# Layer 1's feed-forward in rounds of scores, full products and values, and patches loaded image by image

## The chip, the cores and the metric

The kernel runs on one NeuronCore of one Trainium2 chip. A core has five engines that run beside each other: TensorE (PE in the profile; its weight loads are PEld), VectorE (DVE), ScalarE (ACT), GpSimd (POOL) and SyncE (SP, which here only starts transfers). Matmuls read SBUF and write PSUM, which has eight banks of 512 float32 columns on 128 partitions. The metric is the time on the device, in microseconds, from the first to the last instruction of the program; the median of three runs of the kernel before is 2376.61 us (2375.67 to 2379.23).

## The reference

A small vision model on 32 images of 3 x 256 x 256 in float32. Each image becomes 256 tokens of 256 features (16 x 16 patches times a 768 x 256 matrix), and then passes two layers, each an attention and a feed-forward with a residual. The change touches the tokenizer and the feed-forward of layer 1, which is itself an attention: four heads of 64 features, with four experts each. Cut to what matters:

```python
h = patches @ W.T + b                                   # tokenizer, 32 x 256 tokens
...                                                     # layer 0, attention of layer 1
x = layernorm(h)
sx = x @ hl_w.T + hl_b                                  # 4 heads (n) of 64 features
q  = sx @ wq.T                                          # 4 experts (e) for each head
k, v = sx @ wk.T, sx @ wv.T
scores = q @ k.T * sqrt(64) + causal                    # 256 x 256 for each n and e
out = softmax(scores) @ v
gs  = softmax(concat_e(out) @ gate_w.T + gate_b)        # weight of each expert
mixed = sum_e out * gs
hn  = layernorm(mixed + resid)                          # over 64 features
hx  = relu(hn @ fc1_w.T + fc1_b) @ fc2_w.T + fc2_b
y   = layernorm(hx + hn)
fg  = softmax(y @ fgate_w.T)                            # weight of each head
h   = h + y * fg
```

## The kernel before

The program is written in steps; a scheduler places the instructions on the engines, roughly in program order. All matmuls are float32 and go through one helper, `mm(o, lhsT, rhs)`, so the profile shows one line (L113) for them all; tile names tell them apart. A float32 matmul leaves two records.

The tokenizer takes two images at a time, and all weights of layer 0 are loaded beside the first patches, on another queue:

```python
tokW = load(pw, "tokW")
row_a = load_rows(pw, "rows_a", ...)
wuv = load(wpool_b, "wuv")                # and rows_b, wo, rows_c, w1, w2, before, places
...
def unit_a(b0):
    x = px.tile([P, n_k, 2 * N], F32, name="patch")                 # three buffers
    nc.sync.dma_start(x, patches[:, :, b0 * N : (b0 + 2) * N])
    for j in range(2):
        p = bank()
        for c in range(NC):
            for k in range(n_k):
                mm(p[:, c * D : (c + 1) * D], x[:, k, o : o + P], tokW[:, k, :], k == 0, k == n_k - 1)
        ...                                # bias, statistics of the rows
```

After each half of the images `finish_a` makes the row factors of 16 images at once, on VectorE and with square roots on ScalarE.

In layer 1's feed-forward an image passes through numbered steps, and six images are under way at a time, six steps apart. `prep` makes the operands, `scores` and `weights` the exponentials, `values` the weighted sums, `post` the rest:

```python
def prep(b, im, i):
    # i == 0: normalise, transpose          -> im.xT
    # i == 1: 4 matmuls of 256 columns      -> im.sx (ScalarE)
    # i in (2, 3): 4 matmuls of 256 with A  -> im.g  (half ScalarE, half VectorE)
    # i == 4: 4 matmuls of 168 columns      -> im.v ("ev", VectorE), count of zeros in sx

def scores(im, k):                          # k = 0..5; 64 partitions: two matmuls side by side
    hp, part = k // 3, k % 3
    for h in range(2):
        s, p = slice(h * HD, (h + 1) * HD), bank()
        if part < 2:
            mm(p, im.sx[s, hp, 0:P], im.g[s, hp, 2 * part : 2 * part + 2, :])
        else:
            mm(p, im.sx[s, hp, P:N], im.g[s, hp, :, P:N])

def weights(im, k):                         # mask on VectorE, exponential on ScalarE -> "et"
    for h in range(2):
        nc.vector.tensor_tensor(own, own, over(tri, [P, n_e, P], 1), ALU.add)
        nc.scalar.activation(t.rearrange("p e n -> p (e n)"), p, AF.Exp)

def values(im, j):                          # 64 output partitions: two matmuls side by side
    for n, c in (((2 * hp, 0), (2 * hp + 1, 0)), ((2 * hp, 1),), ((2 * hp + 1, 1),))[part]:
        p = bank()
        for e in range(NE):
            for m in range(c + 1):
                for q in (slice(0, HD), slice(HD, P)):
                    mm(p[q, e * VC : (e + 1) * VC], t[:, q], im.v[:, m, n * VC : (n + 1) * VC], m == 0, m == c)
        nc.scalar.copy(im.o[:, c * NH + n, 0 : NE * VC], p[:, 0 : NE * VC])
```

`VC` is 84: 64 columns of the head, and for each of the four experts four gate logits and a one, which gives the denominator. Every expert's product carries all 84.

```python
def post(b, im, i):
    # 0..2: denominators ("rden"), gates; at 2 GpSimd multiplies all outputs by the gates ("eo")
    # 3..5: sum of experts ("two", "er"), squares, factor by a power on GpSimd ("hv"), scaling
    # 6..8: transposes, fc1 ("hx"), fc2 with the centring matrix ("ey"), squares
    # 9..13: factor, scaling, transposes ("foT"), gate product ("fo_w"), "fout", store

PREP, POST = 6, 15
for t in range(6 * (B - 1) + POST + 14):
    active = [(b, t - 6 * b) for b in range(B) if 0 <= t - 6 * b < POST + 14]
    # for all active images: scores at i = 6..11, then post at 15..28, prep at 0..5,
    # weights at 6..11, values at 9..14
```

So each of the six steps of an image has scores of one image (two matmuls of 512 columns), full 128 x 128 products, and 16 value matmuls.

Of the kernel before, what the change touches and what calls it, by code (L numbers as in the profile page):

```python
# [37 lines left out]
P = 128  # L40
# [11 lines left out]
for _name, _k in [  # L52
    ("b_u", 4), ("b_base", 1), ("gamma", 2), ("beta", 2), ("b1", 8), ("bk1", 2), ("bq1", 2),
    ("bk2", 1), ("bq2", 1), ("ln_w", 2), ("ln_b", 2), ("hl_b", 2), ("fc1_b", 1), ("freq", 1),
    ("e_g", 1), ("e_b", 1), ("fn_g", 1), ("fn_b", 1),
]:
    COLS[_name] = (_n, _k)
    _n += _k
# [12 lines left out]
ROWS_B, N_ROWS_B = _rows(("b_v", 512), ("b_o", 256), ("g", 1))  # L71
# [7 lines left out]
def vit_tower(tc, a, out):  # L79
# [21 lines left out]
    def load_rows(pool, name, at, n):  # L101

        t = pool.tile([P, n], F32, name=name)
        nc.scalar.dma_start(t, a[name].partition_broadcast(P))
        return lambda x: t[:, at[x][0] : at[x][0] + at[x][1]]
# [89 lines left out]
    late = []  # L195

    def phase(unit, images, finish=None, every=1):

        active, step = [], 0
        todo = list(range(0, B, images))
        while todo or active:
            if todo and step % every == 0:
                b = todo.pop(0)
                active.insert(0, (b, unit(b)))
            step += 1
            for b, g in list(active):
                if next(g, g) is not g:  # L210
                    continue
                active.remove((b, g))
                while late:
                    late.pop(0)()
                if finish is not None and (b + images) % HALF == 0:
                    late.append(lambda k=b // HALF: finish(k))
# [7 lines left out]
    with tc.tile_pool(name="a_w", bufs=1) as pw, tc.tile_pool(name="a_x", bufs=3) as px:  # L224
        tokW = load(pw, "tokW")
        row_a = load_rows(pw, "rows_a", ROWS_A, N_ROWS_A)
        wuv = load(wpool_b, "wuv")
        row_b = load_rows(wpool_b, "rows_b", ROWS_B, N_ROWS_B)
        wo = load(wpool_b, "wo")
        row_c = load_rows(wpool, "rows_c", ROWS_C, N_ROWS_C)  # L230
        w1 = load(wpool, "w1")
        w2 = load(wpool, "w2")
        before = load(wpool, "before")
        places = load(wpool, "places")
        st_b = new_stats("b")
        n_k = tokW.shape[1]
        patches = a["patches"].rearrange("(k p) t -> p k t", p=P)

        def unit_a(b0):
            x = px.tile([P, n_k, 2 * N], F32, name="patch")  # L240
            nc.sync.dma_start(x, patches[:, :, b0 * N : (b0 + 2) * N])
            for j in range(2):
                b = b0 + j
                p = bank()
                for c in range(NC):
                    for k in range(n_k):
                        o = j * N + c * P
                        mm(p[:, c * D : (c + 1) * D], x[:, k, o : o + P], tokW[:, k, :], k == 0, k == n_k - 1)
                nc.vector.tensor_tensor(
                    H[b], p.rearrange("p (c d) -> p c d", c=NC), over(row_a("tok_b"), [P, NC, D], 1), ALU.add  # L250
                )
                st, _, i = at(st_b, b)
                for c in range(NC):
                    stats(st, i, c, H[b][:, c, :])
            yield

        def finish_a(k):


            st, rs = st_b[k]  # L260
            n = HALF * NC
            var = st.rearrange("p i c s -> p (i c) s")[:, :, 1]
            low = spool.tile([P, n], F32, name="low")
            v = rsqrt(low, var, 1e-5)
            nc.vector.scalar_tensor_tensor(low, low, 1e-5, v, ALU.mult, ALU.mult)
            s = spool.tile([P, n], F32, name="root")
            nc.scalar.activation(s, var, AF.Sqrt)
            nc.vector.tensor_scalar(s, s, 1e-18, None, ALU.max)
            r = spool.tile([P, n], F32, name="root_r")
            nc.vector.reciprocal(r, s)  # L270
            nc.vector.tensor_mul(r, r, var)
            nc.vector.tensor_add(s, s, r)
            nc.vector.scalar_tensor_tensor(s, s, 0.5, low, ALU.mult, ALU.max)
            nc.vector.reciprocal(r, s)
            nc.vector.tensor_scalar(rs, r, row_b("g"), None, ALU.mult)

        phase(unit_a, 2, finish_a)
# [95 lines left out]
    VC = HD + NE * (NE + 1)  # L373
    OC = NE * (VC + NE + 1)

# [49 lines left out]
    def prepare():  # L425
# [14 lines left out]
        for t in (A, WV, ones_row, fc2):  # L440
            nc.gpsimd.memset(t, 0.0)
        nc.gpsimd.memset(
            ones_row.rearrange("p (n x) -> p n x", n=NH)[:, :, HD:VC]
            .rearrange("p n (e x) -> p n e x", e=NE)[:, :, :, NE : NE + 1], 1.0,
        )
# [15 lines left out]
        for i in range(2):  # L461
# [4 lines left out]
            for hp in range(2):  # L466
                w = WV[s, hp, i * VC : (i + 1) * VC]
                nc.vector.tensor_copy(w[:, 0:HD], wv_i[s, hp, :])
                nc.vector.tensor_copy(
                    w[:, HD:].rearrange("p (e x) -> p e x", e=NE)[:, :, 0:NE],  # L470
                    pv[s, hp * 16 : hp * 16 + 16].rearrange("p (e x) -> p e x", e=NE),
                )

# [291 lines left out]
    with (  # L765
        tc.tile_pool(name="e_1", bufs=1, reuse_waits="tile") as p1,
        tc.tile_pool(name="e_2", bufs=2, reuse_waits="tile") as p2,
        tc.tile_pool(name="e_4", bufs=4, reuse_waits="tile") as p4,
    ):
        class Image:  # L770
            pass
# [3 lines left out]
        def prep(b, im, i):  # L775
            if i == 0:
                im.xT = features(p2, b)
            if i == 1:
# [10 lines left out]
            if i in (2, 3):  # L789
                hp = i - 2  # L790
# [5 lines left out]
            if i == 4:  # L796
# [12 lines left out]
            if i == 5:  # L809
                im.o = p2.tile([P, NC * NH, OC], F32, name="eo")  # L810

        def scores(im, k):


            hp, part = k // 3, k % 3
            if part == 0:
                im.t = getattr(im, "t", {})
                for h in range(2):
                    im.t[2 * hp + h] = (
                        p4.tile([P, NE, N], F32, name="et0"), p4.tile([P, NE, P], F32, name="et1"),  # L820
                    )
            im.p = []
            for h in range(2):
# [5 lines left out]
                im.p.append(p)  # L829

        def weights(im, k):

            hp, part = k // 3, k % 3
            for h in range(2):
                p, n_e = im.p[h], 4 if part == 2 else 2
                own = p.rearrange("p (e n) -> p e n", e=n_e)[:, :, 0:P]
                nc.vector.tensor_tensor(own, own, over(tri, [P, n_e, P], 1), ALU.add)  # L837
                t0, t1 = im.t[2 * hp + h]
                t = t1 if part == 2 else t0[:, 2 * part : 2 * part + 2, :]
                nc.scalar.activation(t.rearrange("p e n -> p (e n)"), p, AF.Exp)  # L840

        def values(im, j):
            hp, part = j // 3, j % 3
            for n, c in (((2 * hp, 0), (2 * hp + 1, 0)), ((2 * hp, 1),), ((2 * hp + 1, 1),))[part]:
                p = bank()
                t0, t1 = im.t[n]
                for e in range(NE):
                    for m in range(c + 1):
                        t = t1[:, e, :] if m else t0[:, e, c * P : (c + 1) * P]
                        for q in (slice(0, HD), slice(HD, P)):  # L850
                            mm(p[q, e * VC : (e + 1) * VC], t[:, q], im.v[:, m, n * VC : (n + 1) * VC], m == 0, m == c)
                nc.scalar.copy(im.o[:, c * NH + n, 0 : NE * VC], p[:, 0 : NE * VC])  # L852
# [26 lines left out]

        def post(b, im, i):  # L880
            if i == 0:
                by_e = im.o.rearrange("p g (e x) -> p g e x", e=NE)
                im.rden = spool.tile([P, NC * NH, NE], F32, name="rden")
                nc.vector.reciprocal(im.rden, by_e[:, :, :, HD + NE])
                nc.vector.scalar_tensor_tensor(good, im.rden, 1.0 / LOW, good, ALU.is_le, ALU.mult)
                nc.vector.scalar_tensor_tensor(good, im.rden, 1.0 / HIGH, good, ALU.is_ge, ALU.mult)
                lg = spool.tile([P, NC * NH, NE, NE], F32, name="lg")
                nc.vector.tensor_tensor(
                    lg, by_e[:, :, :, HD : HD + NE], over(im.rden, [P, NC * NH, NE, NE], 3), ALU.mult
                )  # L890
# [6 lines left out]
            if i == 2:  # L897
                softmax_rest(im.gate, NC * NH)
                nc.vector.tensor_tensor(im.gate, im.gate, im.rden, ALU.mult)  # L899
                im.by_e = im.o[:, :, 0 : NE * VC].rearrange("p g (e x) -> p g e x", e=NE)[:, :, :, 0:HD]  # L900
                nc.gpsimd.tensor_tensor(  # L901
                    im.by_e, im.by_e, over(im.gate, [P, NC * NH, NE, HD], 3), ALU.mult
                )
            if i == 3:
                two = p1.tile([P, NC * NH, 2, HD], F32, name="two")
                nc.vector.tensor_tensor(two, im.by_e[:, :, 0:2, :], im.by_e[:, :, 2:4, :], ALU.add)  # L906
                im.r = p2.tile(G8, F32, name="er")
# [12 lines left out]
            if i == 6:  # L920
                p = feature_major(im.r.rearrange("p (c n) d -> p c (n d)", c=NC))
                im.fT = p2.tile([P, 2, N], F32, name="fxT")
# [3 lines left out]
            if i == 7:  # L926
# [3 lines left out]
                im.hx = p2.tile([P, 2, N], F32, name="hx")  # L930
# [5 lines left out]
            if i == 8:  # L936
# [6 lines left out]
                im.r = p2.tile(G8, F32, name="ey")  # L943
# [4 lines left out]
            if i == 11:  # L948
                p = feature_major(im.r.rearrange("p (c n) d -> p c (n d)", c=NC))
                im.fT = p2.tile([P, 2, N], F32, name="foT")  # L950
# [16 lines left out]
            if i == 13:  # L967
                softmax_rest(im.gate, NC)
                y = p2.tile([P, NC, D], F32, name="fout")
# [10 lines left out]

        images = [Image() for _ in range(B)]
        PREP, POST = 6, 15
        for t in range(6 * (B - 1) + POST + 14):
            active = [(b, t - 6 * b) for b in range(B) if 0 <= t - 6 * b < POST + 14]
            for b, i in active:
                if PREP <= i < PREP + 6:
# [406 lines left out]
```

## Time and profile before

| stage | from, us | to, us |
|---|---|---|
| tokenizer | 13.2 (first matmul) | 182.1 |
| layer 0, attention and feed-forward | 182.1 | about 1026 |
| layer 1, attention | about 1026 | about 1400 |
| layer 1, feed-forward | about 1400 | 2376.4 |

The dearest groups of the last stage by the page, whole run (busy time, mean of one):

| group | count | busy us | mean ns |
|---|---|---|---|
| exponentials, ScalarE, 128x512 | 384 | 227.9 | 604 |
| value matmuls, 84 columns | 6144 records | 265.9 | 240 |
| score matmuls, 512 columns | 768 records | 218.6 | 641 |
| mask added, VectorE | 384 | 185.1 | 514 |
| outputs times gates, GpSimd, 128x2048 | 32 | 115.9 | 3620 |

Busy time is the union of the records of a group; matmul records overlap, since the next one starts while the one before is still in the array, so what a matmul costs is read from one start to the next. A wait is put down to the instruction that ended it.

### The profile page before, as it was taken

To read this page: it belongs to the slowest core of one execution; us is meant where nothing else is said; L and a number is where in the kernel's file an instruction comes from. 1 tells how busy PE (TensorE), PEld (TensorE's weight loads), DVE (VectorE), ACT (ScalarE), POOL (GpSimd) and SP (SyncE) were. 2 spreads that over 40 slices of the span, in tenths; PEclk is the share of its full clock that TensorE was granted. 3 is DMA by queue.
4 is the path that set the end of the run, shared out by engine and by line. 5 is a ranking of instruction groups with operands and counts; after the bars stand their busy time and mean duration, and the time that the engine had idled before them with its cause. 6 is when DMAs were issued, how large, how long until landed. Compare 5 with 4: busy or idle time off the path is not lost.

```text
span 2376.4 us, 36348 instructions
## 1 busy us (share of the span) xinstructions
PE 2231.7 (94%) x14878; PEld 1579.3 (66%) x14878; DVE 1384.0 (58%) x3785; ACT 837.7 (35%) x1544; POOL 518.1 (22%) x462
## 2 busy tenths in 40 slices
PE   7999999999988999999999999999999999999995
PEld 6885666666666677666667766666666666666664
DVE  2435333433347666455556555777777777777774
ACT  0003222222211221234334434555555555555552
POOL 0002222211112221043233111222222222222232
PEclk9999999999998999999999999999999999999996
DMA  7530000000010000000000000000000000000000
GB/s 270 158 107 0 1 1 0 1 1 0 1 39 1 1 1 1 1 1 1 1 1 1 1 1 2 10 10 10 10 10 10 10 10 10 10 11 10 10 10 20
DMA packets 25917, 44.68 MB, mean 19 GB/s; under 512 B 1936, under 2 KB 11408, under 8 KB 25360
## 3 DMA queue, kind: packets, MB, share of 16 engines
q1 hardware_dynamic: 23872, 36.00, 4.7%
q10 hardware_dynamic: 1872, 6.29, 0.7%
q8 instruction: 119, 1.95, 0.3%
q14 instruction: 54, 0.44, 0.1%
HBM read 33.90 MB, written 8.39 MB: 18 GB/s over the span
## 4 chain that ended last, share of the span: by engine, by line
PE 70%; DVE 17%; ACT 6%; POOL 5%; issue 1%; DMA 1%; SPq 0%; DVEq 0%; ACTq 0%; POOLq 0%
PE bank L113 66%; POOL hv L858 4%; ACT et L840 3%; DVE bank L837 3%; DVE fout L973 2%; DVE ss L913 2%; DVE two L906 2%; PE bank L186 2%; DVE ev L803 1%; DVE ey L919 1%; DVE er L919 1%; ACT esq L875 1%; DVE g L193 1%; DVE er L909 1%; PE bank L481 1%
## 5 line engine op out<-in xcount | busy, mean ns | idle before, releaser
L840 ACT ACTIVATE et<-bank 128x512 f32<-128x512 f32 x384 | 227.9, 604 | 366.2 <-DVE bank L837 365.5
L113 PEld LDWEIGHTS bank<-ev,et 128*64 128x64 f32 x6144 | 233.8, 137 | 49.6 <-issue 34.0
L113 PE MATMUL bank<-ev,et 128*64 128x84 f32 x6144 | 265.9, 240 | 0.0
L113 PE MATMUL bank<-g,sx 64*128 64x512 f32 x768 | 218.6, 641 | 0.5 <-ACT et L840 0.3
L901 POOL TENSOR_TENSOR eo<-eo,gate 128x2048 f32<-128x2048 f32 x32 | 115.9, 3620 | 369.5 <-DVE gate L899 358.8
L837 DVE TENSOR_TENSOR bank<-bank,w_tri 128x256 f32<-128x256 f32 (+1 forms) x384 | 185.1, 514 | 14.1 <-PE bank L113 14.1
L113 PE MATMUL bank<-w_tokW,patch 128*128 128x256 f32 x768 | 169.1, 384 | 13.2 <-DMA patch<-in_patches_dram 13.2
L113 PEld LDWEIGHTS bank<-w_tokW,patch 128*128 128x128 f32 x768 | 148.1, 193 | 33.8 <-DMA patch<-in_patches_dram 13.2
L113 PE MATMUL bank<-sx,A 128*128 128x256 f32 x512 | 126.0, 390 | 35.6 <-ACT sx L785 35.6
L113 PE MATMUL bank<-bxT,w_wuv 128*128 128x512 f32 x320 | 146.9, 598 | 4.9 <-ACT bxT L191 4.8
L332 DVE TENSOR_TENSOR bv<-bank,rows_b 128x512 f32<-128x512 f32 x64 | 44.3, 692 | 157.9 <-PE bank L113 157.9
L113 PEld LDWEIGHTS bank<-sx,A 128*128 128x128 f32 x512 | 93.2, 192 | 56.8 <-ACT sx L785 43.5
L852 ACT COPY eo<-bank 128x336 f32<-128x336 f32 x256 | 108.7, 440 | 51.2 <-PE bank L113 48.6
L113 PE MATMUL bank<-w_w,hT 128*128 128x256 f32 x512 | 115.8, 379 | 0.0
L113 PE MATMUL bank<-xsel,w_w 128*128 128x512 f32 x256 | 114.1, 600 | 0.0
L113 PE MATMUL bank<-w_wo,gT 128*128 128x256 f32 x512 | 113.1, 379 | 0.0
L113 PE MATMUL bank<-attn,bv 128*128 128x256 f32 x512 | 113.1, 379 | 0.0
L113 PE MATMUL bank<-w_wuv,bxT 128*128 128x512 f32 x256 | 112.5, 592 | 0.0
L113 PEld LDWEIGHTS bank<-attn,bv 128*128 128x128 f32 x512 | 97.3, 190 | 19.6 <-issue 7.2
L113 PEld LDWEIGHTS bank<-w_wo,gT 128*128 128x128 f32 x512 | 97.3, 190 | 13.2
L858 POOL TENSOR_TENSOR hv<-hv,minus_half 128x8 f32<-128x8 f32 x64 | 104.7, 1636 | 5.3
L113 PEld LDWEIGHTS bank<-w_w,hT 128*128 128x128 f32 x512 | 95.5, 190 | 12.4 <-issue 0.5
(239 smaller groups left out, 3943.1 us busy)
## 6 DMA issues: line engine op xcount, KB each, us to landing
patch<-in_patches_dram SPq DMA_DIRECT2D x16, 1536.0 KB, 7.2
out_dram<-fout SPq DMA_DIRECT2D x32, 256.0 KB, 2.1
w_w<-in_w_dram ACTq DMA_DIRECT2D x2, 1024.0 KB, 13.2
w_wuv<-in_wuv_dram ACTq DMA_DIRECT2D x1, 1152.0 KB, 14.8
w_tokW<-in_tokW_dram ACTq DMA_DIRECT2D x1, 768.0 KB, 9.1
w_wo<-in_wo_dram ACTq DMA_DIRECT2D x1, 512.0 KB, 16.8
rows_b<-in_rows_b_dram ACTq DMA_DIRECT2D x1, 384.5 KB, 15.5
rows_e<-in_rows_e_dram ACTq DMA_DIRECT2D x1, 296.0 KB, 4.3
```

The source lines that it names most:

```text
L113: nc.tensor.matmul(o, lhsT, rhs, start=first, stop=last)
L186: nc.tensor.transpose(p[:, o : o + P], x[:, c, k * P : (k + 1) * P], ident)
L332: nc.vector.tensor_tensor(v, p, row_b("b_v"), ALU.add)
L837: nc.vector.tensor_tensor(own, own, over(tri, [P, n_e, P], 1), ALU.add)
L840: nc.scalar.activation(t.rearrange("p e n -> p (e n)"), p, AF.Exp)
L852: nc.scalar.copy(im.o[:, c * NH + n, 0 : NE * VC], p[:, 0 : NE * VC])
L858: nc.gpsimd.tensor_tensor(v, v, minus_half, ALU.pow)
L901: nc.gpsimd.tensor_tensor(im.by_e, im.by_e, over(im.gate, [P, NC * NH, NE, HD], 3), ALU.mult)
L906: nc.vector.tensor_tensor(two, im.by_e[:, :, 0:2, :], im.by_e[:, :, 2:4, :], ALU.add)
L913: nc.vector.tensor_reduce(ss, im.sq, AX.X, ALU.add)
L919: nc.vector.tensor_tensor(im.r, im.r, over(im.rs, G8, 2), ALU.mult)
L973: nc.vector.scalar_tensor_tensor(y[:, c, s], im.po[c][:, o : o + HD], im.gate[:, c, n : n + 1], H[b][:, c, s], ALU.mult, ALU.add,)
```

## The change

It has three parts. In the feed-forward of layer 1 two score steps are taken together at even steps, and values at odd ones, so that an image has three rounds of scores, exponentials, full products and values where it had six steps; values take the exponentials of rounds before, which 16 single buffers hold. The preparing and the finishing steps are placed further apart (sx at 2, its products at 4 and 6, values' operand at 7, post from 17 to 35), and many buffers are single instead of double. Second, the operand of the values is laid out as two experts' columns, the head's 64, two experts' columns, so that a product takes a slice with only what it needs: 74, 69, 69 and 74 columns. This splits two instructions of `post` in two halves. Third, the tokenizer takes one image at a time with six smaller buffers; layer 0's weights are loaded behind the fifth image's patches, on the same queue; and the row factors are made for each two images on GpSimd.

```diff
-    with tc.tile_pool(name="a_w", bufs=1) as pw, tc.tile_pool(name="a_x", bufs=3) as px:
+    with tc.tile_pool(name="a_w", bufs=1) as pw, tc.tile_pool(name="a_x", bufs=6) as px:
 ...
-            x = px.tile([P, n_k, 2 * N], F32, name="patch")
-            nc.sync.dma_start(x, patches[:, :, b0 * N : (b0 + 2) * N])
+            x = px.tile([P, n_k, N], F32, name="patch")
+            nc.sync.dma_start(x, patches[:, :, b * N : (b + 1) * N])
 ...
+            if b == 4:
+                loaded.extend(layer_0_weights())
+            if b % 2:
+                factors_b(b - 1)
 ...
-    VC = HD + NE * (NE + 1)
-    OC = NE * (VC + NE + 1)
+    EC = NE + 1
+    VC = NE * EC + HD
+    TAKE = ((0, 2 * EC + HD), (EC, EC + HD), (2 * EC, EC + HD), (2 * EC, 2 * EC + HD))
+    OC = sum(w for _, w in TAKE)
 ...
         def values(im, j):
-            hp, part = j // 3, j % 3
-            for n, c in (((2 * hp, 0), (2 * hp + 1, 0)), ((2 * hp, 1),), ((2 * hp + 1, 1),))[part]:
+            for n, c in (((0, 0), (1, 0), (0, 1)), ((1, 1), (2, 0), (3, 0)), ((2, 1), (3, 1)))[j]:
 ...
-                            mm(p[q, e * VC : (e + 1) * VC], t[:, q], im.v[:, m, n * VC : (n + 1) * VC], m == 0, m == c)
-                nc.scalar.copy(im.o[:, c * NH + n, 0 : NE * VC], p[:, 0 : NE * VC])
+                            mm(p[q, o : o + w], t[:, q], im.v[:, m, x : x + w], m == 0, m == c)
+                    o += w
+                nc.scalar.copy(im.o[:, c * NH + n, 0:OC], p[:, 0:OC])
 ...
-        PREP, POST = 6, 15
-        for t in range(6 * (B - 1) + POST + 14):
+        SCORES, VALUES = 6, 11
+        POST = {
+            17: 0, 18: 1, 19: 2, 21: 3, 22: 4, 23: 5, 24: 6, 26: 7, 28: 8, 29: 9, 31: 10, 32: 11, 34: 12, 35: 13,
+        }
+        LAST = 36
+        for t in range(6 * (B - 1) + LAST):
 ...
+            if t % 2 == 0:
+                for do in (scores, weights):
+                    for b, i in active:
+                        if SCORES <= i < SCORES + 6:
+                            do(images[b], i - SCORES)
+                            do(images[b], i - SCORES + 1)
             for b, i in active:
-                if PREP <= i < PREP + 6:
-                    scores(images[b], i - PREP)
+                if i in POST:
+                    post(b, images[b], POST[i])
             for b, i in active:
-                if i >= POST:
-                    post(b, images[b], i - POST)
- ...
+                prep(b, images[b], i)
+            if t % 2:
+                for b, i in active:
+                    if VALUES <= i < VALUES + 6:
+                        values(images[b], (i - VALUES) // 2)
```

## The prediction

> **What bounds the kernel now.** I read the shares of busy time first, then the busy time by stage, then one image of the last stage in order of time, then TensorE's waits there.
>
> ```profile
> PE 2231.7 (94%) x14878; PEld 1579.3 (66%) x14878; DVE 1384.0 (58%) x3785; ACT 837.7 (35%) x1544; POOL 518.1 (22%) x462
> ```
>
> TensorE (PE) is busy 94% of the span and no other engine is near it. But the change touches two stages only. From the stage table (stretch, length, then busy time of each engine with its instructions, clock, DMA share, GB/s):
>
> ```profile
> 0.00:13.20 13.20, 0.00 (x0) 0.00 (x0) 1.86 (x2) 0.00 (x0) 2.68 (x14) 1.00 0.87 270
> 13.20:182.10 168.90, 168.90 (x768) 148.20 (x769) 59.78 (x182) 1.73 (x3) 5.36 (x4) 1.00 0.51 167
> 1480.00:2262.00 782.00, 726.66 (x7673) 507.33 (x7671) 581.27 (x1581) 411.79 (x860) 199.05 (x135) 1.00 0.03 10
> 2262.00:2376.40 114.40, 81.51 (x806) 59.18 (x806) 70.22 (x213) 42.14 (x86) 27.72 (x21) 0.81 0.05 16
> ```
>
> The reader is to see: 13.2 us in which TensorE waits for the first patches; 168.9 us of tokenizer with TensorE full; and from about 1400 us on layer 1's feed-forward, the largest stage (some 970 us), where TensorE is busy 93% and VectorE (DVE) 74%.
>
> Each float32 matmul leaves two records (the tokenizer has 384 matmuls and 768 records). In the stretch of 60 to 120 us, 280 such records of 256 columns fill 60 us: 214 ns a record, 0.837 ns a column. That is my price of streaming. Busy time itself cannot be used, since records overlap; starts can. One step of the feed-forward (start, length, engine, group):
>
> ```profile
> 1803.31 1.38 PE L113 MATMUL bank<-ev,et 128*64 128x84 f32 x32
> 1804.62 1.13 PE L113 MATMUL bank<-g,sx 64*128 64x512 f32 x4
> 1805.68 0.66 PE L481 MATMUL bank<-ident,ex 128*128 128x128 f32 x4
> 1806.27 1.38 PE L113 MATMUL bank<-ev,et 128*64 128x84 f32 x32
> ```
>
> Values (128x64 tiles) run two at a time, so 32 records are 16 pairs of 84 columns: 16 x 84 x 0.837 = 1.125 us, but the next group starts 1.31 us later. Scores (64x128 tiles) are 2 pairs of 512 columns: 0.857 us, but take 1.06. The four transposes stream 4 x 128 x 0.837 = 0.43 and take 0.59. So every change of tile shape costs about 0.18 us (0.185, 0.20, 0.16), and a step has three: values to scores, scores to full products, full products to values. An image has six steps, so 18 changes, some 3.3 us.
>
> One image takes 29.05 us (the count of zeros on sx first starts at 1503.4 and last at 2171.6, 24 times: 668.2 / 23). TensorE's waits with a name, in 1600 to 2150 us, which holds 19 images:
>
> ```profile
> PE bank L113 <- ACT sx L785: 23.9, 19, 1.3
> PE bank L113 <- DVE g L193: 14.8, 19, 1.0
> ```
>
> That is 38.7 / 19 = 2.04 us an image: the first A product follows directly on the step that makes sx, and the WV product comes directly after g's copy. The second has a cause of its own:
>
> ```profile
> 1822.37 3.62 POOL L901 TENSOR_TENSOR eo<-eo,gate 128x2048 f32<-128x2048 f32 x1 [10.45 <-DVE gate L899]
> 1823.67 2.34 DVE L871 TENSOR_TENSOR fgate<-fgate,sm_m 128x8 f32<-128x8 f32 x1
> 1825.93 0.68 DVE L193 COPY g<-bank 128x512 f32<-128x512 f32 x1
> ```
>
> An 8-element multiply on VectorE takes 2.34 us because GpSimd (POOL) is in its 3.62 us multiply; it ends when that does, and the copy of g behind it is late for TensorE.
>
> **What the Trainium skill says.** "TensorEngine Tiling (Array Packing)", section "Tiling Modes": "Mode switching requires drain", switching among tiles of one shape does not. The rows above agree: 0.18 us at each switch, and pairs within one shape go through at the stream's price. "TensorE: Matmul & The Clock Gate", section "LDWEIGHTS (loading the stationary operand)": a weight load takes its columns / 1.2 ns, for 64 columns 53 ns by estimate. A record of 71.5 columns streams 60 ns, so narrower values should still be bound by streaming, with little left; the trace shows only the present 84 columns at 70 ns. "SBUF — State Buffer", section "SBUF: two separate sides": the port pair shared by VectorE and GpSimd is an exclusive lock, held for the whole instruction; the 2.34 us agrees.
>
> **The change part by part.**
>
> Narrower values. Every value product now carries 84 columns: 64 of the head and four groups of 5 (four gate logits and the denominator), though an expert needs only its own group. The new layout puts the 64 in the middle and takes 74, 69, 69 and 74 columns: 286 instead of 336, mean 71.5. An image has six steps of 32 value records, 192, which run as 96 pairs: before 96 x 84 x 0.837 = 6.75 us, after 96 x 71.5 x 0.837 = 5.75. Gain 1.0 us an image. The eight copies of values on ACT shrink from 336 to 286 columns, off the path.
>
> Rounds. Scores of two steps run together at an even step, values of two steps at the following odd one, full products between. Three rounds an image with three switches each: 9 instead of 18, 9 x 0.18 = 1.65 us less.
>
> Spacing. sx at 2, its A products at 4 and 6, ev at 7, and post-processing stretched over 17 to 35: the products that waited get at least one step between producer and consumer. Of 2.04 us I expect half to go. I don't count all of it, because VectorE gets tighter: it is busy 581.27 / 782 = 74%, or 21.6 us of 29.05; without the blocked 2.2 us some 19.4 us stay, plus two small instructions more (a second reciprocal and a second multiply at 0.35 and 0.28). In a 25.4 us image that is 78%. The work is also uneven. By my count of the listed durations, the round that ends with fout and rden has about 9.5 us on VectorE beside 8.6 on TensorE, the others 5 to 6 beside 7 to 8. So masking of the next scores starts late in that round, banks come free late (four of eight hold scores until their exponentials), and TensorE should wait about 1 us an image.
>
> Exponentials. Values now use those of the preceding round; as TensorE waits for no exponential now (the waits above name sx and g alone), this gains nothing by itself; it only keeps rounds of two steps from creating such a wait.
>
> New image: 29.05 - 1.0 - 1.65 - 1.05 = 25.35 us.
>
> Over the stage: 27 image periods run at full rate now; the last four take 26.2, 19.2, 18.5 and 15.9 us between their outputs. After, the chain from an image's first to last step is 36 steps instead of 29, so one more period is spent filling or draining, at perhaps 12 to 15 us, while one full period fewer is paid. I reckon the stage at 114 (fill, 35 steps) + 26 x 25.35 + 84 (the five draining periods) = 857 us, against 107 + 27 x 29.05 + 80 = 971 now: 114 us less. Fill and drain are estimates from these spacings, uncertain by 15 us.
>
> Tokenizer by image. The first transfer is 768 KB instead of 1.5 MB, and the 4.6 MB of layer 0's weights no longer share the DMA with it but follow the fifth image. Until TensorE's start cols, tokW, rows_a and patch 0, and about as much of later patches, some 1.8 MB, must land. The DMA moved 270 GB/s on average up to 13.2 us with a slow first 3 us (86 GB/s, then 231 and 391 in stretches of 3 us): about 8.3 us. Gain 5 us. Image 5's patch stands behind 10.4 MB; by 30 us the DMA has moved 10.3 MB now (stretches of 3 and 5 us, at up to 412 GB/s), and TensorE wants that patch at 8.3 + 1 + 5 x 5.18 = 35 us, so no new wait. Row factors per pair of images on GpSimd replace the two batches on VectorE and ACT, whose square roots force table loads at the start of layer 0's attention (three of 1.28 us near 185 to 190 us): perhaps 1 us. Gain in all 6.
>
> Sum: 2376.6 - 114 - 6 = 2257 us.
>
> **The rivals.** (a) VectorE becomes the bound. If its 19.4 to 20 us suffer more collisions with GpSimd (the multiply is now two of about 1.8 us, so each block is shorter, but there are two) or its uneven round is not made up, the image stays near 27 us: 114 + 26 x 27 + 84 = 900 for the stage, total about 2300. For it: 78% in strict order with many short dependences; against it: ACT and VectorE have 8 us of slack in every image now, and values no longer need the exponentials of the same round. (b) PSUM banks become the bound: four score banks, two fo banks held until fout, three value banks in one round. TensorE would wait at values and at the next scores; the time would be 2290 to 2330. For it: eight banks in all; against it: no wait for a bank among the named waits now, and exponentials take 4 x 0.6 us of an 8 us round. (c) Everything hides: waits go to 0.3 us, image 24.6 us, total about 2235. (d) Weight loads bind the narrow values: no gain of 1.0 us, total about 2285.
>
> **Range and chances.** All gains lie on TensorE, which sets the time; 1.0 + 1.65 us an image are counts times measured prices and hard to lose together, 1.05 is a judgement. To lose 2% (end above 2329) the image must stay above 28 us, which takes rival (a) or (b) in full. I say 2257 us, 2205 to 2312 eight times in ten; faster by over 2% 0.88, within 0.09, slower 0.03.
>
> **What would show it right or wrong.** In the changed profile: value groups of 64 records, 32 pairs, at 60 ns a pair, 1.9 us (rival d: 70 ns); three runs of scores an image with eight records each and nine switches; an image period near 25.4 us; the wait for sx gone; VectorE near 78%. Waits of TensorE for ACT or VectorE at scores or values would show (b), VectorE above 85% (a). The first matmul should start near 8 us with no wait for patches later. I would be wrong most if the drain after the last image grew by more than 30 us or if the rounds' order were not kept on TensorE.

## The result, and the profile after

| | median, us | runs | ratio to before, 95% interval |
|---|---|---|---|
| before | 2376.62 (2375.67 to 2379.23) | 4 | 1 |
| changed | 2300.45 (2300.07 to 2300.85) | 4 | 0.9678 [0.9661, 0.9695] |

The changed kernel is 76 us faster, where 120 were predicted: inside the range, at the value that the first rival named. First the page's shares and then the stage table of the changed kernel (stretch, length, busy time of each engine with its instructions, clock, DMA share, GB/s):

```profile
PE 2138.1 (93%) x14878; PEld 1552.1 (68%) x14878; DVE 1344.1 (58%) x3857; ACT 810.5 (35%) x1538; POOL 587.0 (26%) x573
```

```profile
0.00:9.60 9.60, 0.02 (x1) 0.05 (x1) 0.00 (x0) 0.08 (x1) 3.14 (x29) 1.00 0.80 262
9.60:177.10 167.50, 167.50 (x771) 147.23 (x772) 62.89 (x201) 1.20 (x1) 41.81 (x64) 1.00 0.54 175
1480.00:2190.00 710.00, 636.66 (x7528) 479.50 (x7524) 536.49 (x1605) 381.85 (x840) 221.35 (x158) 1.00 0.03 11
2190.00:2298.40 108.40, 73.57 (x796) 56.23 (x796) 69.41 (x231) 41.48 (x89) 32.53 (x26) 0.85 0.06 19
```

The tokenizer begins 3.6 us earlier and stays full. In the feed-forward TensorE, full 93% of the time before, is now full 636.66 / 710 = 90%: an image takes 27.0 us from one output to the next, not 25.35. TensorE's named waits, 1550 to 2100 us, some 20 images (us in total, times, longest):

```profile
PE bank L111 <- ACT g L189: 33.4, 20, 1.7
PE bank L111 <- ACT et L824: 22.7, 20, 1.1
```

The old waits are gone and two new ones have come: 1.67 us an image before the first scores, for the copy of g, and 1.14 us before the WV product, for a bank that an exponential frees. Together 2.81 us, where the kernel before waited 2.04 and I had predicted 1.0. This is how they stand in time (start, length, engine, line, operation, and in brackets the idle time before and what ended it):

```profile
1808.04 3.81 POOL L895 TENSOR_TENSOR eo<-eo,gate 128x1024 f32<-128x1024 f32 x2 [10.99 <-DVE sm_m L848]
1808.47 2.21 PE L111 MATMUL bank<-ev,et 128*64 128x74 f32 x64
1808.84 1.16 DVE L856 TENSOR_TENSOR fgate<-fgate,sm_m 128x8 f32<-128x8 f32 x1
1810.42 0.68 DVE L938 TENSOR_TENSOR ey<-bank,b_row 128x512 f32<-128x512 f32 x1
1811.20 0.63 ACT L860 ACTIVATE esq<-ey 128x512 f32<-128x512 f32 x1 [2.79 <-DVE ey L938]
1811.73 0.57 ACT L189 COPY g<-bank 128x512 f32<-128x512 f32 x1
1812.35 1.99 PE L111 MATMUL bank<-g,sx 64*128 64x512 f32 x8 [1.67 <-ACT g L189]
...
1813.36 1.21 DVE L900 TENSOR_TENSOR two<-eo 128x1024 f32<-128x1024 f32 x1
1813.53 1.12 POOL L842 TENSOR_SCALAR hv<-ss 128x8 f32<-128x8 f32 x1 [1.68 <-DVE ss L907]
1814.74 1.64 POOL L843 TENSOR_TENSOR hv<-hv,minus_half 128x8 f32<-128x8 f32 x1
1816.41 0.69 DVE L913 TENSOR_TENSOR ey<-ey,hv 128x512 f32<-128x512 f32 x1 [1.73 <-POOL hv L843]
1817.12 0.43 DVE L822 TENSOR_TENSOR bank<-bank,w_tri 128x256 f32<-128x256 f32 x1
1817.58 1.57 ACT L824 ACTIVATE et<-bank 128x512 f32<-128x512 f32 x3 [4.38 <-DVE bank L822]
1818.23 0.98 PE L111 MATMUL bank<-WV,sx 128*128 128x168 f32 x5 [1.14 <-ACT et L824]
```

Read the upper half from below. TensorE waits for ScalarE's copy of g. A's products for it came before the values, which began at 1808.47; but on ScalarE the copy stands behind esq, which waits for VectorE's ey, which stands behind a gate multiply of eight elements that takes 1.16 us because GpSimd is in its multiply. In the lower half the masks of the next scores (`w_tri`) stand on VectorE behind a scaling that waits 1.73 us for GpSimd's power; the power came late because the small instruction before it took 1.12 us where 0.2 is usual, until VectorE's sum `two` was over. Without masks no exponentials, and without these no bank for WV.

So my theory was: neither chain is an amount of work. Both are strict order within an engine behind an instruction that waits for GpSimd, or for the port it shares with VectorE. The rivals were VectorE's amount of work (a), too few banks (b), and values that don't gain from fewer columns (d).

### The profile page after: what moved, and what is told of

The parts are those of the page before. It is cut to its first block, busy times and chain, and to the rows that moved or that the text cites. A ratio compares the mean times of both kernels' runs of the same rounds, so it can differ in the third digit from the quotient of the medians.

```text
span 2298.4 us, 36574 instructions
## 1 busy us (share of the span) xinstructions
PE 2138.1 (93%) x14878; PEld 1552.1 (68%) x14878; DVE 1344.1 (58%) x3857; ACT 810.5 (35%) x1538; POOL 587.0 (26%) x573
## 4 chain that ended last, share of the span: by engine, by line
PE 59%; DVE 20%; ACT 11%; POOL 7%; issue 2%; DMA 1%; SPq 0%; ACTq 0%; DVEq 0%; POOLq 0%
PE bank L111 57%; ACT et L824 5%; POOL hv L843 5%; DVE bank L822 4%; DVE fout L967 2%; DVE ss L907 2%; POOL hv L842 2%; PE bank L184 2%; DVE fgate L856 1%; DVE ey L913 1%; DVE er L913 1%; ACT sx L777 1%; ACT foT L945 1%; DVE junk L797 1%; ACT fxT L917 1%
## 5 line engine op out<-in xcount | busy, mean ns | idle before, releaser
L824 ACT ACTIVATE et<-bank 128x512 f32<-128x512 f32 x384 | 218.9, 599 | 295.9 <-DVE bank L822 295.7
L111 PE MATMUL bank<-g,sx 64*128 64x512 f32 x768 | 193.4, 617 | 46.5 <-ACT g L189 43.6
L111 PEld LDWEIGHTS bank<-ev,et 128*64 128x64 f32 x6144 | 198.6, 137 | 30.1 <-ACT et L824 10.0
L895 POOL TENSOR_TENSOR eo<-eo,gate 128x1024 f32<-128x1024 f32 x64 | 121.9, 1925 | 368.9 <-DVE sm_m L848 305.7
L111 PE MATMUL bank<-ev,et 128*64 128x74 f32 (+1 forms) x6144 | 213.3, 227 | 1.3 <-DVE ey L938 1.1
L111 PEld LDWEIGHTS bank<-g,sx 64*128 64x128 f32 x768 | 71.0, 185 | 99.2 <-ACT g L189 48.0
L189 ACT COPY bxT<-bank 128x512 f32<-128x512 f32 x16 | 9.4, 585 | 335.1 <-PE bank L184 335.1
```

The lines of the kernel that those rows point to most:

```text
L111: nc.tensor.matmul(o, lhsT, rhs, start=first, stop=last)
L824: nc.scalar.activation(t, p, AF.Exp)
L895: nc.gpsimd.tensor_tensor(im.mix[k], im.mix[k], over(im.gate[:, :, 2 * k : 2 * k + 2], [P, NC * NH, 2, HD], 3), ALU.mult)
```

## The experiments

Each kernel ran beside runs of the kernel before on the same chip (medians 2376.1 to 2378.0). "Period" is the spacing of outputs in the middle of the feed-forward.

| kernel | us | ratio to before, 95% | period, us |
|---|---|---|---|
| narrow values alone | 2324.67 | 0.9776 [0.9760, 0.9792] | 27.2 |
| GpSimd's multiply halved alone | 2330.3 | 0.9799 [0.9783, 0.9815] | 27.4 |
| changed, 84 columns again | 2310.5 | 0.9720 [0.9704, 0.9736] | 27.2 |
| changed, no zero counts | 2301.32 | 0.9681 [0.9665, 0.9697] | 27.0 |
| changed, gates on ScalarE | 2281.22 | 0.9598 [0.9582, 0.9614] | 26.2 |
| changed, scaling on GpSimd | 2227.18 | 0.9369 [0.9353, 0.9385] | 24.3 |
| changed, both cures | 2212.89 | 0.9308 [0.9292, 0.9323] | 23.84 |
| gates on ScalarE, prep first | 2366.22 | 0.9948 [0.9932, 0.9965] | 29.2 |
| both cures, 84 columns | 2245.04 | 0.9440 [0.9424, 0.9456] | 24.84 |
| both cures, six steps | 2265.79 | 0.9530 [0.9514, 0.9546] | 25.5 |
| both cures, old tokenizer | 2213.14 | 0.9308 [0.9292, 0.9323] | 23.84 |

### Is it the amount of VectorE's work?

```diff
-                nc.vector.tensor_scalar(
-                    junk, im.sx.rearrange("p h n -> p (h n)"), 0.0, 0.0, ALU.is_equal, ALU.add,
-                    accum_out=zeros[:, b : b + 1],
-                )
```

and the same for `fT`. This leaves out the counting of zeros by which the kernel decides on a slower general path.

> The changed kernel without the two counts of zeros (leaves out the check for zeros, 2 x 0.77 us of VectorE an image, which stand on neither of the two chains I see). If VectorE's amount of work is the bound (rival a): 1.5 us an image less, total about 2260 us. My theory, order and waits and not the amount: within 10 us of 2300.

Measured: 2301.3 us, 1 us from the changed kernel, with the same two waits to a tenth of a microsecond. Rival (a) as an amount falls: two instructions of together 1.5 us of VectorE an image went for nothing (VectorE's busy time between 1550 and 2050 us fell from 377.9 to 354.9 us).

### The first chain: one multiply of eight elements

```diff
-            nc.vector.tensor_tensor(x, x, over(m, [P, g, 4], 2), ALU.mult)
+            if g == NC:
+                for c in range(NC):
+                    nc.scalar.activation(x[:, c, :], x[:, c, :], AF.Copy, scale=m[:, c : c + 1])
```

> The changed kernel with the head gates' last multiply (8 elements, blocked 1.16 us by GpSimd's multiply) on ScalarE, as two instructions of 4 elements. My theory: VectorE's ey comes about 1 us earlier, so ScalarE's square and copy of g too, and TensorE's wait for g falls from 1.67 to about 0.7 us: total about 2274 us. Rival, banks or exponentials set the pace: no change, 2300 us.

Measured: 2281.2 us. TensorE's waits of this kernel, 1550 to 2100 us:

```profile
PE bank L111 <- ACT et L824: 37.2, 21, 1.8
```

The wait for g went entirely (1.67 us, more than I expected), and the second one grew from 1.14 to 1.77: a part of what one chain releases the other takes. The period fell by 0.8 us.

### The second chain: the scaling behind the power

```diff
-                nc.vector.tensor_tensor(im.r, im.r, over(im.rs, G8, 2), ALU.mult)
+                nc.gpsimd.tensor_tensor(im.r, im.r, over(im.rs, G8, 2), ALU.mult)
```

> The changed kernel with the scaling of er and ey by their row factors on GpSimd, where the factor is made, instead of VectorE. My theory of the second wait: masks of the next scores stand on VectorE behind this scaling, which waits for GpSimd's power, which waits for the port that VectorE's sum of experts holds; so exponentials and the bank for WV come 1.14 us late. Then that wait goes, and the one for g (1.67 us) stays: about 26.0 us a period, total about 2272 us. Rival, the banks are too few whatever the order: the wait stays, 2300 us.

Measured: 2227.2 us, well beyond the 2272 that I expected. The wait for the bank went, and of the wait for g 0.4 us an image is left:

```profile
PE bank L111 <- ACT g L189: 8.9, 23, 0.7
```

I had taken the chains for independent. They are not: the gate multiply is blocked as long as in the changed kernel (1.16 us), but ey now begins 7.2 us after the round's first scores (1794.74 to 1801.92 in this trace) and not 8.5 (1801.95 to 1810.42), so VectorE's earlier lateness was part of the wait for g. The number of banks is the same as before, so the wait for a bank was one of order (rival b as it was put falls).

### Both cures

> Both cures together: head gates' last multiply on ScalarE and the scalings of er and ey on GpSimd. If the two waits are all that was lost against the prediction's image: 26.2 - 1.8 = 24.4 to 25 us a period, total 2232 to 2250 us, and no named wait of TensorE above 0.5 us an image. Rival, a further bound (GpSimd's 11 us an image with its long chain, or banks): 26 us, 2275 us.

Measured: 2212.9 us, and in five more runs 2211.6, against 2300.45. This beats both kernels. The stage table for 500 us in its middle, and one round on TensorE:

```profile
1550.00:2050.00 500.00, 500.00 (x6001) 377.71 (x6001) 395.15 (x1218) 329.34 (x713) 227.32 (x168) 1.00 0.04 13
```

```profile
1815.50 2.21 PE L111 MATMUL bank<-ev,et 128*64 128x74 f32 x64
1817.64 1.99 PE L111 MATMUL bank<-g,sx 64*128 64x512 f32 x8
1819.56 0.66 PE L470 MATMUL bank<-ident,er 128*128 128x128 f32 x4
1820.05 1.89 PE L111 MATMUL bank<-sx,A 128*128 128x256 f32 x8
1821.78 0.60 PE L470 MATMUL bank<-ident,ex 128*128 128x128 f32 x4
1822.22 1.31 PE L111 MATMUL bank<-WV,sx 128*128 128x168 f32 x8
1823.45 2.21 PE L111 MATMUL bank<-ev,et 128*64 128x74 f32 x64
```

The trace shows no gap of TensorE in 500 us, though VectorE is 79% busy, which I had thought too tight. GpSimd still makes the power and still collides with `two`; only nothing that TensorE needs stands behind it:

```profile
1818.29 1.22 DVE L904 TENSOR_TENSOR two<-eo 128x1024 f32<-128x1024 f32 x1
1818.47 1.13 POOL L842 TENSOR_SCALAR hv<-ss 128x8 f32<-128x8 f32 x1 [0.89 <-DVE ss L911]
1819.67 1.66 POOL L843 TENSOR_TENSOR hv<-hv,minus_half 128x8 f32<-128x8 f32 x1
1819.76 0.42 DVE L822 TENSOR_TENSOR bank<-bank,w_tri 128x256 f32<-128x256 f32 x1
```

The masks begin at 1819.76, while the power is still running, and not 0.7 us after its end.

### What the columns are worth

The changed kernel with all columns:

```diff
-    TAKE = ((0, 2 * EC + HD), (EC, EC + HD), (2 * EC, EC + HD), (2 * EC, 2 * EC + HD))
+    TAKE = ((0, VC),) * NE
```

> The changed kernel with all 84 columns in each value product again (rounds kept). If narrow values gain on TensorE in each of the three rounds: period 27.0 to 28.0 us, total about 2328 us. My theory says that in two of the three rounds TensorE waits after the values or before them for a chain on other engines (g's copy 1.67 us, a bank freed by an exponential 1.14 us), which does not get longer: then the longer values eat the waits, the period rises by 0.3 to 0.5 us, total about 2310 us.

Measured: 2310.5 us, 27.2 us a period, as my theory had it. Its waits show where the columns went: g's fell to 17.2 us over 20 images (0.86 each, from 1.67), the bank's stayed.

```profile
PE bank L111 <- ACT et L824: 23.6, 21, 1.1
PE bank L111 <- ACT g L189: 17.2, 20, 1.1
```

With both cures, where nothing can absorb them:

> The kernel with both cures (2213 us, 23.8 us an image, no named wait of TensorE) with all 84 columns in each value product again. There TensorE is full, so each column costs: 96 pairs x 12.5 columns x 0.837 ns = 1.0 us an image, 24.85 us a period, total about 2241 us. Rival, the price of a pair is not its columns: 2213 us.

Measured: 2245.0 us; the period rose from 23.84 to 24.84, by the 1.0 us that the price of a column gives. TensorE is full with all columns too:

```profile
1550.00:2050.00 500.00, 500.00 (x5764) 381.57 (x5760) 383.92 (x1168) 321.30 (x683) 220.79 (x163) 1.00 0.04 12
```

Rival (d) falls: a pair of 71.5 columns is bound by its columns.

The narrow layout in the kernel before:

> The kernel before with the narrow value products alone (286 instead of 336 columns, six steps an image, two-image patches). If values are bound by streaming, as the prediction says: 1.0 us an image less on TensorE, 29.05 to about 28.05 us a period, total about 2347 us. If weight loads bind them (rival d): period unchanged, about 2376 us. If the two waits of the old schedule grow by what the values save: in between.

Measured: 2324.7 us, 53 us less and not 29. That was too good, and it came from something else in the edit: the new layout also cuts GpSimd's multiply of 2048 elements in two.

```diff
-                nc.gpsimd.tensor_tensor(
-                    im.by_e, im.by_e, over(im.gate, [P, NC * NH, NE, HD], 3), ALU.mult
-                )
+                for k in range(2):
+                    e = slice(2 * k, 2 * k + 2)
+                    nc.gpsimd.tensor_tensor(
+                        im.by_e[:, :, e, :], im.by_e[:, :, e, :],
+                        over(im.gate[:, :, e], [P, NC * NH, 2, HD], 3), ALU.mult
+                    )
```

> The kernel before with GpSimd's gate multiply cut into two halves and nothing else (84 columns, six steps). The narrow layout alone gave 53 us where 29 were expected; I think the surplus is not the columns but the halved multiply, which blocks VectorE's small gate multiply 0.7 instead of 2.3 us, so that TensorE's wait for g's second half (0.77 us, with its restart about 0.9) goes. Then this gives 29.05 to about 28.2 us a period, total about 2350 us. Rival, the columns did it all: 2376 us.

Measured: 2330.3 us by the cut alone, beyond my 2350. The small gate multiply and the wait left over in this kernel:

```profile
L871 DVE TENSOR_TENSOR fgate<-fgate,sm_m x18: 632/634/637, 1559.0 to 2024.7; 128x8 f32<-128x8 f32 x18
```

```profile
PE bank L113 <- ACT sx L785: 12.2, 19, 0.6
```

Blocked 0.63 instead of 2.34 us, it no longer holds up g: that wait (0.78) is gone, and the one for sx fell from 1.26 to 0.64. Narrow values on top of it gain only 5.6 us, because the wait for sx grows again to 31.1 / 21 = 1.48 us:

```profile
PE bank L113 <- ACT sx L791: 31.1, 21, 1.5
```

### What the rounds are worth

Six steps an image with narrow values and both cures (and the old tokenizer):

> Six steps an image as in the kernel before, with narrow values and both cures, two-image patches: what are rounds worth once the waits are gone? Nine more switches of the tile shape at 0.16 to 0.18 us and what is left of the wait for sx (0.6 to 1.5 us): 23.8 + 1.6 + 0.6 to 1.5 = 26.0 to 26.9 us a period; with 3.5 us of tokenizer and a longer drain total 2290 to 2315 us. Rival, switches cost nothing when TensorE is full: 24 to 24.5 us a period, about 2240 us.

Measured: 2265.8 us, better than I expected, as no wait for sx is left. TensorE is full in this kernel too:

```profile
1550.00:2050.00 500.00, 500.00 (x5628) 353.84 (x5625) 359.38 (x1123) 306.72 (x667) 191.72 (x158) 1.00 0.04 12
```

So its period, 25.5 against 23.84, shows the nine extra switches alone: 1.66 us, 0.18 us each.

### A failed improvement: operands first

```diff
             for b, i in active:
+                prep(b, images[b], i)
+            for b, i in active:
                 if i in POST:
                     post(b, images[b], POST[i])
-            for b, i in active:
-                prep(b, images[b], i)
```

> The changed kernel with the head gates' last multiply on ScalarE, and prep ahead of post within a step, so that A's products and g's copies come before fc2 and the gates. This moves g's copies early but leaves the masks behind the scaling: if the second chain (scaling behind the power) is the one left, its wait of 1.8 us stays and the time is as with the first cure alone, about 2281 us; if it was the order of prep and post that mattered, about 2240 us.

Measured: 2366.2 us, 85 us worse than without it; neither theory had that. TensorE and the VectorE instructions it depends on:

```profile
1809.19 3.81 POOL L899 TENSOR_TENSOR eo<-eo,gate 128x1024 f32<-128x1024 f32 x2 [10.27 <-DVE gate L896]
1811.86 1.13 PE L111 MATMUL bank<-g,sx 64*128 64x512 f32 x4
1813.03 1.23 DVE L904 TENSOR_TENSOR two<-eo 128x1024 f32<-128x1024 f32 x1 [3.05 <-POOL eo L899]
1814.69 0.68 DVE L942 TENSOR_TENSOR ey<-bank,b_row 128x512 f32<-128x512 f32 x1
1815.42 1.60 PE L111 MATMUL bank<-g,sx 64*128 64x512 f32 x4 [2.44 <-DVE ey L942]
```

The scheduler has put `two`, which needs GpSimd's multiply, ahead of ey. VectorE stands idle 3.05 us, ey keeps its bank, and the second half of the scores waits for that bank. It is the same kind of chain at a third place, and here too it ends in a bank.

The wait itself is less than half of the loss. The period is 3.0 us longer than with the gates on ScalarE alone (29.2 against 26.2), but TensorE's named wait grew only from 1.8 to 2.9 us an image (52.6 / 18 from 1550 to 2050 us). Most of the rest is a lower granted clock (the third figure from the end of the first line):

```profile
1550.00:2050.00 500.00, 446.39 (x4866) 327.72 (x4866) 332.41 (x1025) 260.09 (x581) 127.31 (x103) 0.92 0.03 10
1816.95 3.17 PE L111 MATMUL bank<-sx,A 128*128 128x256 f32 x8
```

The eight A products behind the wait take 3.17 us, and 1.89 in the kernel with both cures. TensorE is busy 26.1 us an image (446.39 / 500 x 29.2) and not 24.4 (466.41 / 500 x 26.2), for the same products. All 18 waits of this stretch, 2.4 to 3.3 us each, are followed by such slow products; of the 19 waits of 1.8 us with the gates on ScalarE alone one is, and the clock there is 1.00. That the longer wait brings the clock down fits this, but no run tests it.

### The tokenizer

Both cures with the tokenizer of the kernel before:

> The kernel with both cures, with the tokenizer of the kernel before (two images at a time, weights of layer 0 beside the first patches, factors in two batches). The trace of the changed kernel shows the first matmul 3.6 us earlier, and from layer 0's feed-forward on everything 3.5 us earlier: total about 2216.5 us. If the prediction's 6 us were right after all: 2219 us.

Measured: 2213.1 us (2210.9 to 2213.9), no different from 2212.9 (2208.1 to 2215.7).

> The kernel with both cures once more, in more rounds, since its four runs were spread over 7.6 us and so can't be told from the one with the tokenizer of before (2213.1 us), though the two traces stand 4.6 us apart. If the tokenizer by image is worth the 3.5 to 4.6 us of the traces: 2207 to 2210 us. If not: 2213 us.

Measured: 2211.6 us (2208.9 to 2215.6). The runs of this kernel spread by more than the effect, so the totals don't separate the two tokenizers; the profiles show the first matmul at 9.1 and 9.6 us with the new one and at 13.0 with the old. Even that lead doesn't last in every trace: at the start of layer 1's attention (first transpose of `dx`) the two traces with the new tokenizer are at 1021.6 and 1024.4 us, and the one with the old at 1025.0.

## Why the prediction was right or wrong

**Price of a column, price of a switch: right.** 1.0 and 1.65 us an image were predicted, 1.00 and 1.66 measured where TensorE is full.

**Spacing: the step that failed.** "Of 2.04 us I expect half to go" was the term mis-sized: 2.81 us were measured in its place. 29.05 - 1.0 - 1.65 + (2.81 - 2.04) = 27.2, and 27.0 was measured; the 1.65 us between 27.0 and the predicted 25.35, times 26 periods, is 43 us, as much as the whole miss (the smaller errors below cancel). The two waits I knew did go. The order of VectorE was the right place to look: I expected masks that start late and banks that come free late. But I treated the rest as a smaller leftover of them, and did not follow the order on ScalarE and VectorE to see what would stand in front of g's copy and of the masks. I named VectorE's tightness and the banks as causes; the amount had no part (2301.3 us without 1.5 us of it), and the bank was the end of a chain, not its start.

**The two halves of GpSimd's multiply.** I had shown the 2.34 us block in the kernel before and that g's copy stood behind it, and had the cut in the diff, but entered it only as a risk ("but there are two"). It alone gives 46 us in the old schedule, the largest single effect of the change there. The three parts don't add up: cut, then narrow values, then rounds and tokenizer gave 46, 6 and 24 us in that order; with both cures, columns give 32 us, and six steps with the old tokenizer cost 53.

**Rivals.** (a) was right in its number, 2300, and half right in its cause: it named collisions with GpSimd, and both chains have one in them; but it let them add to VectorE's work, and the amount had no part. (b) was wrong for the changed kernel, whose wait for a bank went with the same number of banks. The signs set for the two didn't separate them: TensorE waited for ScalarE at the scores, with VectorE at 536.49 / 710 = 76% and not above 85%, which was to show (b). And the argument against (b), that no named wait in the kernel before was for a bank, misread the second of the two waits:

```profile
1826.67 1.41 PE L113 MATMUL bank<-WV,sx 128*128 128x168 f32 x8 [0.77 <-DVE g L193]
```

The WV product doesn't read g; by its operands it can only have waited for the bank that g's copy empties. (c) and (d) were wrong.

**Fill and drain.** 84 us were reckoned for the last five periods; 25.7 + 15.5 + 17.7 + 8.1 + 11.3 = 78 were measured (from one image's first `fout` to the next). The fill was reckoned 7 us longer than before; the first output leaves at 1516.0 us and not at 1508.7, and with the 3.5 us of lead that is some 11 us longer.

**Tokenizer.** 6 us were predicted. The first matmul came at 9.6 us, not 8.3, and at the start of layer 1's attention the trace is 3.5 us ahead. In the totals it can't be told from nothing.

## What to carry to other kernels

Where one engine sets the time, what a change is worth depends not only on the work it removes but on what then stands in front of the instruction that this engine waits for: follow that chain back through every engine's own order, and ask of each link whether it waits for GpSimd. A tiny VectorE instruction with both inputs in SBUF can cost what is left of the GpSimd instruction beside it (here 2.34 us for eight elements, where a like one just ahead of GpSimd's took 0.17); cut the long one, or move the small one. And look at the granted clock before a loss is put down to a wait alone. And price savings with the waits gone: the same columns were worth 10 us before the cures and 32 after.

## What the runs showed of the hardware

The block between VectorE and GpSimd works both ways: VectorE's 128x8 multiply took 2.34, 1.16 or 0.63 us by where it met GpSimd's, and GpSimd's 128x8 multiply-add took 1.12 us beside VectorE's `two`, against 0.2 alone. VectorE instructions that read a bank were not held: ey took its usual 0.68 us while GpSimd multiplied (1808.04 to 1811.85). That agrees with the exclusive lock in the Trainium skill's "SBUF — State Buffer", section "SBUF: two separate sides", for operations with two inputs in SBUF. Scaling 128x512 took 1.04 to 1.48 us on GpSimd against 0.69 on VectorE, and was still the better place for it.
